# Two adapter layers over 128 samples on one core: the ends of the last two pairs of samples shared out anew between VectorE, GpSimd, ScalarE and TensorE

## The chip, the core and the metric

The program runs on one core of a Trainium2 chip. A core has TensorE (PE in the profile; its weight loads are PEld), VectorE (DVE), ScalarE (ACT), GpSimd (POOL) and SyncE (SP), which issues most of the DMAs; ScalarE can issue them too. Each engine works through its own list of instructions in order, and they wait for one another by semaphores. The metric is the device time of one execution in microseconds (us). Before the change three executions took 3142.12, 3143.81 and 3145.17 us, so the median is 3143.81 us.

## What is computed

The input x holds 128 samples of 128 rows by 1024 columns in f32, and each sample has a role that picks one of three sets of weights. Two layers of the same form follow one another:

```python
h = jnp.einsum('bsh,bhk->bsk', hidden_states, W_down[role]) + b_down[role][:, None, :]
h = jax.nn.gelu(h, approximate=False)
u = jnp.einsum('bsk,bkh->bsh', h, W_up[role]) + b_up[role][:, None, :]
y = hidden_states + u
mean = jnp.mean(y, axis=-1, keepdims=True)
var = jnp.mean(jnp.square(y - mean), axis=-1, keepdims=True)
yn = (y - mean) * jax.lax.rsqrt(var + LN_EPS)
return yn * gamma[role][:, None, :] + beta[role][:, None, :]
```

H is 1024 and K is 512. What matters here is the last part, the layer norm: a row's mean and variance, then (y - mean) * gamma * 1/sqrt(var + eps) + beta.

## The kernel before

There are four phases: down and up of layer 0, then down and up of layer 1. A phase runs over 64 items of two samples each. An item of two samples with one role computes its product in seven parts, each a product of two halves, instead of eight (Winograd's form of a 2 x 2 block product); the last item of the program is such a pair, and so is the one before it. A phase's products go into three kinds of PSUM bank, "b" (3 buffers), "e" (3) and "a" (2). ScalarE puts the bias into a bank first (`seeded`), and the products add to it with start=False.

The order of all work is written by hand. Each step is pushed on a heap with a due time in slots (`at`), an item's base being 7 slots after that of the item before; the steps are emitted in order of due time, and each engine keeps the order in which its instructions were emitted. So the due times in `finish` and `finish_last` decide what stands before what on each engine.

In the up phase the seven parts of an item are evicted on VectorE: `begin` (L629) adds a bank to x, `whole` and `end` (L635 for the last item, L638 for the others) add the second part to it and, for the others, sum the row as well. For the last item BN_STATS (L636) takes the statistics.

An item's end for all but the last (`finish`), for each of its two samples s:

- `squares`: on ScalarE the mean (L700, L702), the sum of squares (L704, an ACTIVATE over 128x1024) and the variance (L705); on GpSimd the power -1/2 of it (L706), which gives the factor v.
- `scaled`: on VectorE o = (x + mean) * gamma (L709; here "mean" is the negative mean).
- `stored`: for s = 0 o * v on ScalarE (L716) and + beta on GpSimd (L717); for s = 1 both in one instruction on VectorE (L719). Then the store of 512 KB on SP's queue.

The last item's end (`finish_last`): `total` joins the statistics (L654) and adds eps (L656) on VectorE and takes the power on GpSimd (L657); `scaled` (L660) gives o for both samples on VectorE, 1024 columns each; `stored` (L666) applies v and beta to half a sample on VectorE and stores 256 KB, for both halves of sample 1 and the right half of sample 0; `stored_beside` does the left half of sample 0 on ScalarE (L671) and GpSimd (L672), with the store on ScalarE's queue.

The item before the last is number 61 in the program's names, the last is 62. On VectorE the tail of the list, as emitted, is: L638 (61, its last part), L629 (62), L709 (61, sample 1), L635 (62, part 5), L636, L719 (61, sample 1), L635 (62, part 6), L636, L654, L656, L635 (62, part 7), L636, L654, L656, L660 twice, L666 three times. Part 7 uses the same PSUM bank as part 5, so its products wait for the eviction of part 5.

Of the kernel before, what the change touches and what calls it, by code (L numbers as in the profile page):

```python
# [26 lines left out]
def kernel(  # L27
# [57 lines left out]
    def flat(tag, bufs, name, size=2048):  # L85
        return work.tile([P, size], F32, tag=tag, name=name, bufs=bufs)
# [177 lines left out]
    def zeros(tags):  # L264
        for t in tags:
            ps = psum.tile([P, 512], F32, tag=t, name=f"{t}_zero", bufs=3)
            nc.tensor.matmul(ps, zero[:, 0:P], zero[:, P:640], start=True, stop=True)
# [55 lines left out]
    def gathered(name, values, where):  # L323

        ps = bank_a(name + "_ps")
        n = where.shape[1]
        nc.tensor.matmul(ps[0:SQ, 0:n], values, where, start=True, stop=True)
        t = const.tile([1, n], I32, name=name)
        nc.vector.tensor_copy(t, ps[0:1, 0:n])
        return t  # L330
# [15 lines left out]
    counted(own_place, key, own_key, ALU.is_gt, ones_r)  # L346
    nc.vector.tensor_copy(wide_place, own_place.to_broadcast((P, SQ)))
    place = gathered("place", wide_place, onehot)
    zeros("bbbeeebbb")

    def reg(t, s, engines, top):
# [21 lines left out]
    def result(i, y, cols, queue):  # L373


        dst = out[ds(i, 1), :, cols].rearrange("o s h -> (o s) h")
        store = queue.dma_start(dst, y).ins
        tc.declare_no_dep(store, group="result", reason="disjoint rows")
        tc.add_to_no_dep_group("result", store)
# [197 lines left out]
    class Up:  # L577
# [63 lines left out]

        whole = end

        def finish_last(self):


            mv = [const.tile([P, 3], F32, name=f"last_mv{s}") for s in range(2)]
            o = [flat("q", 4, f"o{self.tag}_{s}", H) for s in range(2)]
            row = lambda t, s, cols: t[:, ds(self.places[s], 1), cols].rearrange("p o n -> p (o n)")
            self.out_at = [reg(perm, 2 * self.n + s, [ENG.SP, ENG.Activation], B - 1) for s in range(2)]  # L650
            left, right, both = slice(0, H // 2), slice(H // 2, H), slice(0, H)

            def total(s):
                nc.vector.bn_aggr(mv[s][:, 0:2], self.stat[:, s])  # L654
                v = mv[s][:, 2:3]
                nc.vector.tensor_scalar(v, mv[s][:, 1:2], LN_EPS, None, ALU.add)  # L656
                nc.gpsimd.tensor_tensor(v, v, mhalf[:, 0:1], ALU.pow)  # L657

            def scaled(s):
                nc.vector.scalar_tensor_tensor(  # L660
                    o[s], self.x[:, s], mv[s][:, 0:1], row(self.ph.gamma, s, both), ALU.subtract, ALU.mult
                )

            def stored(s, cols, queue):
                y, v = o[s][:, cols], mv[s][:, 2:3]
                nc.vector.scalar_tensor_tensor(y, y, v, row(self.ph.beta, s, cols), ALU.mult, ALU.add)  # L666
                result(self.out_at[s], y, cols, queue)

            def stored_beside():
                y, v = o[0][:, left], mv[0][:, 2:3]  # L670
                nc.scalar.mul(y, y, v)  # L671
                nc.gpsimd.tensor_tensor(y, y, row(self.ph.beta, 0, left), ALU.add)  # L672
                result(self.out_at[0], y, left, nc.scalar)

            return [
                (10.2, lambda: total(0)),
                (12.2, lambda: total(1)),
                (12.4, lambda: scaled(0)),
                (12.5, lambda: scaled(1)),
                (12.6, lambda: stored(1, left, nc.sync)),  # L680
                (12.7, lambda: stored(1, right, nc.sync)),
                (12.8, stored_beside),
                (12.9, lambda: stored(0, right, nc.sync)),
            ]

        def finish(self):
            if self.last:
                return self.finish_last()
            steps = []
            for s in range(2):  # L690
                t = (10.4, 12.4)[s] if self.n < NPAIR else (10.9, 12.65)[s]
                one = lambda n: small.tile([P, 2], F32, tag=n, name=n + self.tag, bufs=6)
                box = {}
                row = lambda t, s=s: t[:, ds(self.places[s], 1), :].rearrange(
                    "p o n -> p (o n)"
                )

                def squares(s=s, box=box, one=one):
                    part, box["m"], box["v"] = one("part"), one("mean"), one("var")
                    nc.scalar.mul(part, self.stat[:, s], -1.0 / H)  # L700
                    m, v = box["m"][:, 0:1], box["v"][:, 0:1]
                    nc.scalar.activation(m, part[:, 0:1], AF.Identity, bias=part[:, 1:2])  # L702
                    box["o"] = flat("q", 4, f"o{self.tag}_{s}", H)
                    nc.scalar.activation(box["o"], self.x[:, s], AF.Square, bias=m, accum_out=v)  # L704
                    nc.scalar.activation(v, v, AF.Identity, bias=eps, scale=1.0 / H)  # L705
                    nc.gpsimd.tensor_tensor(v, v, mhalf[:, 0:1], ALU.pow)  # L706

                def scaled(s=s, box=box, row=row):
                    nc.vector.scalar_tensor_tensor(  # L709
                        box["o"], self.x[:, s], box["m"][:, 0:1], row(self.ph.gamma), ALU.add, ALU.mult  # L710
                    )

                def stored(s=s, box=box, row=row):
                    o, v = box["o"], box["v"][:, 0:1]
                    if s == 0:
                        nc.scalar.mul(o, o, v)  # L716
                        nc.gpsimd.tensor_tensor(o, o, row(self.ph.beta), ALU.add)  # L717
                    else:
                        nc.vector.scalar_tensor_tensor(o, o, v, row(self.ph.beta), ALU.mult, ALU.add)  # L719
                    if self.layer == 0:  # L720
                        nc.sync.dma_start(mid[self.n][s], o)
                    else:
                        i = reg(perm, 2 * self.n + s, [ENG.SP], B - 1)
                        result(i, o, slice(0, H), nc.sync)

                steps += [(t, squares), (t + 1.3, scaled), (t + 3.1, stored)]
            return steps


    SLOTS = 7  # L730
# [12 lines left out]
    for k, ph in enumerate(phases):  # L743
        for m, n in enumerate(sequence):
# [4 lines left out]
            def load(box=box, ph=ph, n=n, kind=kind, m=m):  # L749
                item = box["item"] = kind(ph, n)  # L750
                item.m = m
                item.early = ph is phases[0] and m == 0
                item.last = ph is phases[-1] and m == NI - 1
                item.among_weights = ph is phases[2] and m < 3
                if m == left_over_at + 1:
                    item.SEED = -1.65
                item.load()
# [151 lines left out]
```

## Time and profile before

| | us |
|---|---|
| median of three runs | 3143.81 |
| the profiled execution | 3143.59 |
| its span (first to last instruction) | 3141.8 |
| PE busy in the span | 3109.3 (99%) |
| DVE, POOL, ACT busy | 1977.3, 1793.9, 1203.6 |
| the last matmul's modelled end | 3128.45 |
| the last VectorE instruction's end | 3138.60 |

The times in the views below count from the span's start. A line of the timeline gives start, duration, engine, line of the code, operation and what it writes and reads; neighbours on one engine with the same line are merged (x2, x3), and in brackets stands how long the engine was idle before it and who ended that. From the last matmul to the end of the span there are 13.4 us.

### The profile page before, as it was taken

The page shows a single profiled execution, that of the slowest core. Times are in us where ns is not written, and L with a number is a line of the kernel's source. Part 1 is how long each engine was busy: PE and PEld are TensorE (multiplying, and loading weights), DVE is VectorE, ACT ScalarE, POOL GpSimd, SP SyncE. Part 2 cuts the span into 40 slices and gives each one's busy share as a digit, 9 for nine tenths or more (in the row PEclk, how much of TensorE's full clock was granted, in tenths as well). Part 3 has the DMA queues.
Part 4 walks back from the last instruction along what each step waited for, and adds up shares of the span by engine and source line. Part 5 has one row for each costly group of instructions (what it writes and reads, how often), then busy time and mean ns, then how long its engine had stood idle before and what let it go on. Part 6 is the DMA issues. An engine that isn't in the chain of part 4 may idle for free.

```text
span 3141.8 us, 42319 instructions
## 1 busy us (share of the span) xinstructions
PE 3109.3 (99%) x10806; PEld 2053.3 (65%) x10806; DVE 1977.3 (63%) x2794; ACT 1203.6 (38%) x2814; POOL 1793.9 (57%) x1396
## 2 busy tenths in 40 slices
PE   8999999999999999999999999999999999999998
PEld 6888888888544444444478888888884444444443
DVE  5655445454578777788854444444447777787777
ACT  1222222222445455555432222222224545554554
POOL 3544444444577767777654443444436777677776
PEclk9999999999999999999999999999999999999999
DMA  8888878886786666666796555555568766666665
GB/s 191 207 209 213 209 206 210 212 213 191 278 286 222 218 217 218 217 223 216 235 260 164 128 135 128 134 125 137 126 184 292 264 219 216 218 217 221 215 226 175
DMA packets 430165, 642.21 MB, mean 204 GB/s; under 512 B 36081, under 2 KB 305906, under 8 KB 428786
## 3 DMA queue, kind: packets, MB, share of 16 engines
q1 hardware_dynamic: 429458, 637.94, 69.1%
q8 instruction: 102, 1.67, 0.2%
q10 hardware_dynamic: 480, 1.57, 0.2%
q14 instruction: 125, 1.02, 0.1%
HBM read 405.01 MB, written 234.36 MB: 204 GB/s over the span
## 4 chain that ended last, share of the span: by engine, by line
PE 48%; DMA 1%; DVE 1%; issue 0%; ACT 0%; DVEq 0%; SPq 0%; ACTq 0%
PE bu L410 14%; PE bd L410 14%; PE eu L410 7%; PE ed L410 7%; PE au L410 3%; PE ad L410 3%; DMA mid<-ou 0%; DVE ou L719 0%; DMA wall<-mid 0%; DMA hd<-hd 0%; ACT ou L704 0%; DVE xu L635 0%; DVE last_stat L636 0%; DVE xu L638 0%; DVEq L905 0%
## 5 line engine op out<-in xcount | busy, mean ns | idle before, releaser
L410 PE MATMUL bu<-wall,hTu 128*128 (+1 forms) x2048 | 922.0, 592 | 2.1 <-POOL ou L717 0.7
L527 DVE STREAM_TRANSPOSE xTd<-xqd 128x1024 f32<-128x1024 f32 x250 | 505.0, 2087 | 354.1 <-PE bd L410 275.4
L410 PEld LDWEIGHTS bu<-wall,hTu 128*128 128x128 f32 x2048 | 388.7, 190 | 490.9 <-issue 455.6
L401 POOL TENSOR_TENSOR Sd<-xTd 128x512 f32<-128x512 f32 x125 | 160.5, 1284 | 802.6 <-DVE xTd L527 798.7
L706 POOL TENSOR_TENSOR varu<-varu,mhalf 128x1 f32<-128x1 f32 x254 | 333.7, 1314 | 383.1 <-ACT varu L705 383.1
L410 PE MATMUL bd<-wall,xTd 128*128 (+1 forms) x2080 | 490.9, 379 | 1.4 <-DMA wall<-T 0.8
L410 PE MATMUL eu<-wall,hTu 128*128 (+1 forms) x1040 | 488.0, 592 | 0.0
L709 DVE SCALAR_TENSOR_TENSOR ou<-xu,meanu,tables 128x1024 f32<-128x1024 f32 x254 | 327.1, 1288 | 253.3 <-ACT ou L704 253.0
L410 PE MATMUL bd<-wall,Sd 128*128 (+1 forms) x2016 | 476.5, 379 | 2.3 <-ACT hd L560 1.6
L410 PEld LDWEIGHTS bd<-wall,xTd 128*128 128x128 f32 x2080 | 394.9, 190 | 58.0 <-issue 3.5
L410 PEld LDWEIGHTS bd<-wall,Sd 128*128 128x128 f32 x2016 | 382.8, 190 | 56.7 <-issue 4.1
L565 ACT ACTIVATE hd<-hd 128x256 f32<-128x256 f32 x382 | 159.4, 418 | 536.4 <-DVE hd L564 536.4
L410 PEld LDWEIGHTS eu<-wall,hTu 128*128 128x128 f32 x1040 | 197.6, 190 | 247.5 <-issue 229.6
L700 ACT ACTIVATE partu<-statu 128x2 f32<-128x2 f32 x254 | 51.9, 204 | 730.6 <-DVE xu L638 730.6
L717 POOL TENSOR_TENSOR ou<-ou,tables 128x1024 f32<-128x1024 f32 x127 | 299.5, 2358 | 0.1
L704 ACT ACTIVATE ou<-xu,meanu 128x1024 f32<-128x1024 f32 x254 | 292.2, 1150 | 8.3
L410 PE MATMUL ed<-wall,xTd 128*128 (+1 forms) x1072 | 254.6, 381 | 4.8 <-DVE xTd L402 4.8
L401 POOL TENSOR_TENSOR hTu<-hTu 128x256 f32<-128x256 f32 x126 | 205.3, 1630 | 66.3 <-DVE hTu L607 54.4
L410 PE MATMUL ed<-wall,Sd 128*128 (+1 forms) x1008 | 238.2, 379 | 0.1
L410 PE MATMUL ad<-wall,xTd 128*128 (+1 forms) x1008 | 238.2, 379 | 0.0
L410 PE MATMUL au<-wall,hTu 128*128 (+1 forms) x504 | 236.8, 592 | 0.0
L410 PEld LDWEIGHTS ed<-wall,xTd 128*128 128x128 f32 x1072 | 204.5, 191 | 33.6 <-issue 5.6
(114 smaller groups left out, 3349.8 us busy)
## 6 DMA issues: line engine op xcount, KB each, us to landing
xqd<-in_x_dram SPq DMA_DIRECT2D x512, 128.0 KB, 3.3
hd<-hd SPq DMA_DIRECT2D x256, 256.0 KB, 2.4
xu<-in_x_dram SPq DMA_DIRECT2D x128, 512.0 KB, 5.0
mid<-ou SPq DMA_DIRECT2D x128, 512.0 KB, 6.1
xu<-mid SPq DMA_DIRECT2D x128, 512.0 KB, 5.8
out_dram<-ou SPq DMA_DIRECT2D x126, 512.0 KB, 5.5
hqu<-hd SPq DMA_DIRECT2D x244, 256.0 KB, 6.5
xqd<-mid SPq DMA_DIRECT2D x488, 128.0 KB, 3.8
```

What stands on the lines that cost most here:

```text
L401: engine.tensor_tensor(dst[:, 1], a11, a21, ALU.subtract)
L410: nc.tensor.matmul(ps[:, 0:cols], a[:, j], w.rhs(r, j, cols), start=start and j == 0, stop=j == n - 1, skip_group_check=True,)
L527: nc.vector.transpose(self.a[:, s].rearrange("p j (t a) -> p j a t", t=SQ), self.xq[s].rearrange("p a (i j) -> p j a i", i=SQ),)
L565: nc.scalar.activation(y, y, AF.Gelu)
L700: nc.scalar.mul(part, self.stat[:, s], -1.0 / H)
L704: nc.scalar.activation(box["o"], self.x[:, s], AF.Square, bias=m, accum_out=v)
L706: nc.gpsimd.tensor_tensor(v, v, mhalf[:, 0:1], ALU.pow)
L709: nc.vector.scalar_tensor_tensor(box["o"], self.x[:, s], box["m"][:, 0:1], row(self.ph.gamma), ALU.add, ALU.mult)
L717: nc.gpsimd.tensor_tensor(o, o, row(self.ph.beta), ALU.add)
```

## The change

The `scaled` and `stored` steps of the last two items are shared out differently.

- Item 61, sample 0: `stored` runs on VectorE in one instruction (L763 after), no longer on ScalarE and GpSimd.
- Item 61, sample 1: (x + mean) runs on ScalarE (L750) and * gamma on GpSimd (L751). For v and beta, ScalarE makes a 128x128 matrix with v on its diagonal (L681, from `same`, an identity matrix made once at the program's start), copies beta into two PSUM banks (L686), and TensorE multiplies the diagonal matrix with each half of o and adds it to the bank (L690). ScalarE copies the two banks back into o (L691) and stores 512 KB on its own queue.
- Item 62, sample 0, left half: `scaled` is done for this half alone on VectorE (L665), then the same three steps follow: a third bank with beta, a second diagonal matrix, one product, one copy and a store of 256 KB on ScalarE's queue.
- Item 62, the rest: `scaled` for sample 1 (1024 columns), its two halves stored, then `scaled` and `stored` for the right half of sample 0, all on VectorE (L665, L672), stores on SP's queue as before.

After the change the tail of VectorE's list is: L640 (61, its last part), L631 (62), L763 (61, sample 0), L637 (62, part 5), L638, L637 (part 6), L638, L659, L661, L637 (part 7), L638, L659, L661, L665 (62, sample 0 left), L665 (sample 1), L672 twice, L665 (sample 0 right), L672. On GpSimd the tail is L746 twice (61's powers), L751, L662 twice. On ScalarE it is L745, L750, L681, L686 three times, L681, L691 twice, a store, L691, a store. TensorE gets the three products after part 7 of item 62. The lists of all engines are otherwise as before, but for `same` at the start of VectorE's.

```diff
--- before.py
+++ after.py
@@ -346,6 +346,8 @@
     counted(own_place, key, own_key, ALU.is_gt, ones_r)
     nc.vector.tensor_copy(wide_place, own_place.to_broadcast((P, SQ)))
     place = gathered("place", wide_place, onehot)
+    same = const.tile([P, P], F32, name="same")
+    nc.vector.tensor_scalar(same, iota_row, iota_col, None, ALU.is_equal)
     zeros("bbbeeebbb")
 
     def reg(t, s, engines, top):
@@ -641,14 +643,17 @@
 
         whole = end
 
+        def row(self, t, s, cols=slice(0, H)):
+            return t[:, ds(self.places[s], 1), cols].rearrange("p o n -> p (o n)")
+
         def finish_last(self):
 
 
             mv = [const.tile([P, 3], F32, name=f"last_mv{s}") for s in range(2)]
-            o = [flat("q", 4, f"o{self.tag}_{s}", H) for s in range(2)]
-            row = lambda t, s, cols: t[:, ds(self.places[s], 1), cols].rearrange("p o n -> p (o n)")
+            o = []
             self.out_at = [reg(perm, 2 * self.n + s, [ENG.SP, ENG.Activation], B - 1) for s in range(2)]
             left, right, both = slice(0, H // 2), slice(H // 2, H), slice(0, H)
+            diagonal, begun = {}, {}
 
             def total(s):
                 nc.vector.bn_aggr(mv[s][:, 0:2], self.stat[:, s])
@@ -656,30 +661,65 @@
                 nc.vector.tensor_scalar(v, mv[s][:, 1:2], LN_EPS, None, ALU.add)
                 nc.gpsimd.tensor_tensor(v, v, mhalf[:, 0:1], ALU.pow)
 
-            def scaled(s):
+            def scaled(s, cols):
                 nc.vector.scalar_tensor_tensor(
-                    o[s], self.x[:, s], mv[s][:, 0:1], row(self.ph.gamma, s, both), ALU.subtract, ALU.mult
+                    o[s][:, cols], self.x[:, s, cols], mv[s][:, 0:1], self.row(self.ph.gamma, s, cols),
+                    ALU.subtract, ALU.mult,
                 )
 
             def stored(s, cols, queue):
                 y, v = o[s][:, cols], mv[s][:, 2:3]
-                nc.vector.scalar_tensor_tensor(y, y, v, row(self.ph.beta, s, cols), ALU.mult, ALU.add)
+                nc.vector.scalar_tensor_tensor(y, y, v, self.row(self.ph.beta, s, cols), ALU.mult, ALU.add)
                 result(self.out_at[s], y, cols, queue)
 
-            def stored_beside():
-                y, v = o[0][:, left], mv[0][:, 2:3]
-                nc.scalar.mul(y, y, v)
-                nc.gpsimd.tensor_tensor(y, y, row(self.ph.beta, 0, left), ALU.add)
-                result(self.out_at[0], y, left, nc.scalar)
+            def room():
+                o.extend(flat("q", 4, f"o{self.tag}_{s}", H) for s in range(2))
+                t = flat("s", 3, "diagonal", 1792)
+                diagonal.update(before=t[:, 0:P], last=t[:, P : 2 * P])
+
+            def on_diagonal(name, v):
+                nc.scalar.mul(diagonal[name], same, v)
+
+
+            def begin_bank(item, s, cols, t):
+                begun[item.n, cols.start] = ps = bank(t, f"{item.tag}_end{cols.start}")
+                nc.scalar.copy(ps, item.row(item.ph.beta, s, cols))
+
+            def by_tensor(item, y, name, cols):
+                ps = begun[item.n, cols.start]
+                nc.tensor.matmul(ps, diagonal[name], y[:, cols], start=False, stop=True, skip_group_check=True)
+                nc.scalar.copy(y[:, cols], ps)
+
+            def begin_banks():
+                begin_bank(before_last[0], 1, left, "b")
+                begin_bank(before_last[0], 1, right, "e")
+                begin_bank(self, 0, left, "b")
+
+            def end_before():
+                item, box = before_last
+                for cols in (left, right):
+                    by_tensor(item, box["o"], "before", cols)
+                i = reg(perm, 2 * item.n + 1, [ENG.Activation], B - 1)
+                result(i, box["o"], both, nc.scalar)
+
+            def end_left():
+                by_tensor(self, o[0], "last", left)
+                result(self.out_at[0], o[0][:, left], left, nc.scalar)
 
             return [
+                (8.6, room),
+                (8.8, lambda: on_diagonal("before", before_last[1]["v"][:, 0:1])),
+                (9, begin_banks),
                 (10.2, lambda: total(0)),
+                (12.05, lambda: on_diagonal("last", mv[0][:, 2:3])),
+                (12.1, end_before),
                 (12.2, lambda: total(1)),
-                (12.4, lambda: scaled(0)),
-                (12.5, lambda: scaled(1)),
+                (12.3, lambda: scaled(0, left)),
+                (12.4, end_left),
+                (12.5, lambda: scaled(1, both)),
                 (12.6, lambda: stored(1, left, nc.sync)),
                 (12.7, lambda: stored(1, right, nc.sync)),
-                (12.8, stored_beside),
+                (12.8, lambda: scaled(0, right)),
                 (12.9, lambda: stored(0, right, nc.sync)),
             ]
 
@@ -691,9 +731,9 @@
                 t = (10.4, 12.4)[s] if self.n < NPAIR else (10.9, 12.65)[s]
                 one = lambda n: small.tile([P, 2], F32, tag=n, name=n + self.tag, bufs=6)
                 box = {}
-                row = lambda t, s=s: t[:, ds(self.places[s], 1), :].rearrange(
-                    "p o n -> p (o n)"
-                )
+                row = lambda t, s=s: self.row(t, s)
+                if self.before_last and s == 1:
+                    before_last[:] = [self, box]
 
                 def squares(s=s, box=box, one=one):
                     part, box["m"], box["v"] = one("part"), one("mean"), one("var")
@@ -706,13 +746,17 @@
                     nc.gpsimd.tensor_tensor(v, v, mhalf[:, 0:1], ALU.pow)
 
                 def scaled(s=s, box=box, row=row):
+                    if self.before_last and s == 1:
+                        nc.scalar.activation(box["o"], self.x[:, s], AF.Identity, bias=box["m"][:, 0:1])
+                        nc.gpsimd.tensor_tensor(box["o"], box["o"], row(self.ph.gamma), ALU.mult)
+                        return
                     nc.vector.scalar_tensor_tensor(
                         box["o"], self.x[:, s], box["m"][:, 0:1], row(self.ph.gamma), ALU.add, ALU.mult
                     )
 
                 def stored(s=s, box=box, row=row):
                     o, v = box["o"], box["v"][:, 0:1]
-                    if s == 0:
+                    if s == 0 and not self.before_last:
                         nc.scalar.mul(o, o, v)
                         nc.gpsimd.tensor_tensor(o, o, row(self.ph.beta), ALU.add)
                     else:
@@ -723,8 +767,13 @@
                         i = reg(perm, 2 * self.n + s, [ENG.SP], B - 1)
                         result(i, o, slice(0, H), nc.sync)
 
-                steps += [(t, squares), (t + 1.3, scaled), (t + 3.1, stored)]
+                steps += [(t, squares), (t + 1.3, scaled)]
+
+                if not (self.before_last and s == 1):
+                    steps.append((t + (3.2 if self.before_last else 3.1), stored))
             return steps
+
+    before_last = []
 
 
     SLOTS = 7
@@ -751,6 +800,7 @@
                 item.m = m
                 item.early = ph is phases[0] and m == 0
                 item.last = ph is phases[-1] and m == NI - 1
+                item.before_last = ph is phases[-1] and m == NI - 2
                 item.among_weights = ph is phases[2] and m < 3
                 if m == left_over_at + 1:
                     item.SEED = -1.65
```

## The prediction

> **What bounds the kernel now.** I read the page first, for which engine sets the time, and then the last 20 us alone, since the change touches nothing else but one instruction at the start.
>
> ```profile
> PE 3109.3 (99%) x10806; PEld 2053.3 (65%) x10806; DVE 1977.3 (63%) x2794; ACT 1203.6 (38%) x2814; POOL 1793.9 (57%) x1396
> ```
>
> TensorE is the bound of the whole, and the change removes none of its products. What it can shorten is the end, after TensorE has nothing left to cover the other engines. The timeline of the end, a choice of lines:
>
> ```profile
> 3124.53 1.28 DVE L709 SCALAR_TENSOR_TENSOR ou<-xu,meanu,tables 128x1024 f32<-128x1024 f32 x1 [1.27 <-ACT ou L704]
> ...
> 3125.73 0.68 DVE L635 TENSOR_TENSOR xu<-bu,xu 128x512 f32<-128x512 f32 x1
> 3126.19 2.35 POOL L717 TENSOR_TENSOR ou<-ou,tables 128x1024 f32<-128x1024 f32 x1
> 3126.45 0.69 DVE L636 BATCH_NORM_STATS2 last_stat<-xu 128x6 f32<-128x512 f32 x1
> ...
> 3126.47 1.98 PE L410 MATMUL bu<-wall,hTu 128*128 x4 [0.56 <-DVE xu L635]
> ...
> 3127.06 2.56 DVE L719 SCALAR_TENSOR_TENSOR ou<-ou,varu,tables 128x1024 f32<-128x1024 f32 x1
> ...
> 3129.55 0.68 DVE L635 TENSOR_TENSOR xu<-eu,xu 128x512 f32<-128x512 f32 x1
> ...
> 3131.30 0.68 DVE L635 TENSOR_TENSOR xu<-bu,xu 128x512 f32<-128x512 f32 x1
> ...
> 3133.12 2.48 DVE L660 SCALAR_TENSOR_TENSOR ou<-xu,last_mv,tables 128x1024 f32<-128x1024 f32 x2
> ...
> 3135.29 1.43 POOL L672 TENSOR_TENSOR ou<-ou,tables 128x512 f32<-128x512 f32 x1 [0.48 <-ACT ou L671]
> 3135.71 2.89 DVE L666 SCALAR_TENSOR_TENSOR ou<-ou,last_mv,tables 128x512 f32<-128x512 f32 x3
> 3136.75 0.40 ACTq L377 DMA_DIRECT2D out_dram<-ou  x1
> ```
>
> Three losses are to be seen. VectorE waits 1.27 us for ScalarE before L709, and the eviction of part 5 (3125.73) stands behind it, so TensorE waits 0.56 us. L719 takes 2.56 us where it takes 1.25 to 1.32 elsewhere (its minimum and median before 3120): it ends 1.1 us after L717 does. The first L666 takes 1.56 us and the other two 0.74 (so its own line's view says): it runs beside L672. And parts 6 and 7, whose products were done at 3125.9 and 3128.45, are evicted at 3129.55 and 3131.30. So from 3125.73 on VectorE's list alone sets the end, as the chain of waits says too, whose last line is
>
> ```profile
> 3137.93 0.66 DVE ou L666
> ```
>
> The windows of 1 us show what lies behind it (engines' busy time, then clock, DMA share, GB/s):
>
> ```profile
> 3130.00:3131.00 1.00, 0.00 (x0) 0.00 (x0) 0.93 (x3) 0.00 (x0) 0.00 (x0) 0.75 1.00 393
> ...
> 3138.00:3139.00 1.00, 0.00 (x0) 0.00 (x0) 0.59 (x1) 0.00 (x0) 0.00 (x0) 0.50 1.03 385
> 3139.00:3140.00 1.00, 0.00 (x0) 0.00 (x0) 0.00 (x0) 0.00 (x0) 0.00 (x0) 0.50 1.04 383
> 3140.00:3141.00 1.00, 0.00 (x0) 0.00 (x0) 0.00 (x0) 0.00 (x0) 0.00 (x0) 0.50 0.42 158
> ```
>
> Stores move about 385 GB/s, the last byte comes at 3140.4, and 1.4 us later the span ends: 3.2 us after VectorE's last instruction.
>
> [...] L719 and L666 (o and the table) are held to the end of L717 and L672; L635 and L636 beside L717 keep 0.68 and 0.69 us. [...] The kernel's biases already work so, at 0.57 us for a copy of 512 columns (L428). [...] Here it goes from 1.00 to 0.75 and 0.50 in the windows from 3130 on, some 2 us after its last product. [...] The three 1 us windows from 3138 move 0.93 MB of both queues together.
>
> **The change, part by part.** I rebuild the end from step lengths in this trace, start to start: L635 to L636 0.72 us, L636 to L654 0.73, L654 to L656 0.24, L656 to L660 0.13, L656 to L635 0.07, L666 to L666 0.67 (512 columns), L660 to L660 1.20 (1024), L660 to the L666 that reads it 1.39, so a dependent step costs 0.19 more.
>
> *Up to part 5's eviction.* L709 goes from VectorE, and with it the 1.27 us wait. In its place comes L763 for sample 0 of item 61. Its o is ready at 3122.04 (L709's first one, 3120.76 + 1.28), its v at 3122.46 (L706, 3121.14 + 1.32), both before L629 ends at 3123.26. So L763 runs 3123.2 to 3124.5. Part 5's products (3122.31, the last at 3123.60, modelled 0.59) are done by 3124.2, so L637 starts at 3124.45: 1.28 us earlier. What queues behind L763 is this eviction, so part 7 and the end: the new wait is for GpSimd's power, with 0.7 us to spare.
>
> *TensorE.* Part 6 starts at 3124.03 as before and takes 4 x 0.43 = 1.72; part 7 then follows at 3125.75 without the wait, modelled end 3127.63 (0.8 us earlier).
>
> *Parts 6 and 7.* L719 and its stall are gone from VectorE. Part 6 can be evicted at 3125.95, then L638 3126.67, L659 3127.40, L661 3127.64. Part 7's eviction follows at 3127.75, not 3131.30. Of the 3.55 us won here 1.28 were counted above, so this is 2.27.
>
> *The last steps.* From there: L638 3128.47, L659 3129.20, L661 3129.44, L665 left half of sample 0 3129.57, L665 sample 1 3130.24, L672 twice at 3131.63 and 3132.30, L665 right half 3132.97, L672 on it 3133.83, end 3134.57 (0.74). That is 6.82 us from part 7's eviction, where before it was 7.30: one L660 of 1.20 becomes two of 0.67, one dependent step adds 0.19, the 0.82 us block by L672 goes. Sum for VectorE: 1.28 + 2.27 + 0.48 = 4.03 us, end at 3134.57 for 3138.60.
>
> *GpSimd and ScalarE beside it.* L750 like L716, 1.13 us: 3124.73 to 3125.87. L751 like L717, 2.35: 3125.95 to 3128.30[...]. The diagonal matrix isn't in the trace; between an ACTIVATE of two columns (L700, 0.20) and 512 columns (L671, 0.72) I take 0.4. Three copies of beta, 0.52 apart, end by 3127.8. The power L662 follows L751, so 3128.9, the second diagonal 3129.35. Hidden, all of it.
>
> *The products.* The start of the program shows that a product of 512 f32 columns is two matmuls of 0.43 us (the zero products of L267: 3 calls, x6), so 0.86 and 0.16 more to its modelled end. 61's halves: 3128.35 to 3129.4, and to 3130.2. Copies back, 0.57 each (PSUM to SBUF for 256 columns is 0.37, L560; 256 columns into PSUM cost the same): 3130.0 and 3130.8. A register load (0.29) and the issue (0.40): the 512 KB start by 3131.5. The third product waits for L665 (3130.3), ends 3131.3, is copied by 3132.2 and issued by 3132.7. Against the last store on SP (3134.6) this has about 1.9 us to spare. At half clock each product takes 1.71 us: the issue is then at about 3135.1, and 0.5 us are lost.
>
> *Stores.* Before, 1 MB followed in the last 2 us of issues; now there are 512 KB and four times 256 KB (1.57 MB) issued from 3131.5 to 3134.6. With data 0.95 us after an issue (3136.75 to 3137.7 before) at 385 GB/s the last byte comes at 3136.4, the span ends 1.4 us later: 3137.8. `same` at the start (0.29, like L277) falls into VectorE's wait of 3.77 us for the first bias, so it is free; without that cover it costs its 0.29 us.
>
> So the span goes from 3141.8 to 3137.8. The profiled execution was 3143.59, 1.8 us more than its span, so it would be 3139.6; the median is 0.2 above it: 3139.8 us, 0.13% faster. A measurement of this kernel tells about 0.2% (6.3 us) from no change, and the shown runs spread over 3 us.
>
> **Rivals.**
>
> *The gain is smaller, about 2.7 us (3141.1).* L661 could be excluded by L751 (to 3128.3: 0.6 us late), the products could run at half clock (0.5), and the stores could go at the 292 GB/s of the busiest slice of the page: 1.57 MB take 5.4 us from 3132.3, so the end is at 3139.1. Against it: no small VectorE instruction in the shown end is held by GpSimd, and the stores alone moved 385.
>
> *Nothing is gained (3143.8, within 1 us).* L719's stall would be one that other executions don't have. Against it: another L719, at 3114.55, takes 2.41 us.
>
> *Slower: GpSimd's power in front of the last product.* Place: L763 at 3123.2, before part 5's eviction. Price: each us that the power of item 61 is later than 3123.2 delays part 7 and all behind it by as much. It decides from 0.7 + 4.0 = 4.7 us of delay, and the time would be 3144.8 at 5.7. For it: GpSimd is in order and L706's powers stand behind L717 of item 60. Against: that one ends at 3115.87.
>
> *More gained than 0.2%.* VectorE needs 6.8 us after part 7 and TensorE can't end earlier, so only chance in the measurement brings this: 3137.2.
>
> **How the numbers follow.** Forecast 0.56, smaller gain 0.24, nothing 0.06, slower 0.04, more than 0.2% 0.10. The range goes from 3137.6 (the forecast with half of the runs' spread and some 0.7 us of step lengths) to 3142.8 (the smaller gain with the same spread). The forecast's own range is 3138.3 to 3141.2. Faster by over 0.2%: 0.10; slower: 0.04; between: 0.86.
>
> **What would show it.** Right: part 7's matmuls without idle time before them; part 7's eviction some 3.5 us earlier; no VectorE instruction above 1.3 us in the last 15; ScalarE's second store issued before SP's last. Wrong: L763 waiting for GpSimd, a long L661, a product that takes 1.7 us, a last byte more than 2 us after the last issue, or a difference in the 3100 us before the end.

## The result, and the profile after

| | median of runs, us | runs |
|---|---|---|
| before, beside it | 3144.57 | 22 |
| after | 3140.40 | 22 |

The ratio is 0.9987 with a 95% interval of 0.9982 to 0.9993: some 4 us faster, 0.13%. One of the 22 runs of after took 8687.84 us, for a reason that no trace shows; it is left out of the ratio, and without it the median is 3140.34. The profiled execution of after took 3142.18 us, its span 3139.98. That execution is on the slow side of the median by 1.8 us, and the reason lies not in the tail, as will be seen. So the tail is measured here from a point inside it: the first product of part 6 of item 62, the last group of products that writes an "e" bank (`eu`) before the end. The distance from there to the end of the span is called the tail below. Before, part 6 started at 3124.03 and the span ended at 3141.82: 17.79 us. After, 3126.57 and 3139.98: 13.41 us.

The busy line of the page of after:

```profile
PE 3115.3 (99%) x10812; PEld 2056.7 (65%) x10812; DVE 1976.0 (63%) x2795; ACT 1204.9 (38%) x2821; POOL 1788.3 (57%) x1395
```

TensorE is still the bound of the whole. Its count is up by six: three products of two matmuls each. The timeline of after's end, a choice of lines (start, duration, engine, line, operation, what it writes and reads, idle time before it):

```profile
3125.71 1.28 DVE L763 SCALAR_TENSOR_TENSOR ou<-ou,varu,tables 128x1024 f32<-128x1024 f32 x1
3126.57 1.88 PE L412 MATMUL eu<-wall,hTu 128*128 x4
3126.90 0.68 DVE L637 TENSOR_TENSOR xu<-bu,xu 128x512 f32<-128x512 f32 x1
...
3128.29 1.88 PE L412 MATMUL bu<-wall,hTu 128*128 x4
...
3128.47 2.35 POOL L751 TENSOR_TENSOR ou<-ou,tables 128x1024 f32<-128x1024 f32 x1 [0.49 <-ACT ou L750]
...
3130.19 0.15 DVE L661 TENSOR_SCALAR last_mv<-last_mv 128x1 f32<-128x1 f32 x1
3130.26 0.68 DVE L637 TENSOR_TENSOR xu<-bu,xu 128x512 f32<-128x512 f32 x1
...
3130.88 1.13 PE L690 MATMUL bu_end<-ou,diagonal 128*128 128x512 f32 x2 [0.71 <-POOL ou L751]
...
3134.14 1.41 DVE L672 SCALAR_TENSOR_TENSOR ou<-ou,last_mv,tables 128x512 f32<-128x512 f32 x2
3134.74 0.38 ACTq L379 DMA_DIRECT2D out_dram<-ou  x1
...
3136.25 0.75 DVE L672 SCALAR_TENSOR_TENSOR ou<-ou,last_mv,tables 128x512 f32<-128x512 f32 x1
```

Part 7 (3128.29) follows part 6 after 1.72 us, with no idle time in brackets; before there were 0.56 us of it. The eviction of part 7 (3130.26) comes 3.69 us after the start of part 6; before, it came 7.27 us after it. L763, which is queued in front of part 5's eviction (3126.90), shows no wait. No VectorE instruction is held: the two L672 take 1.41 us together, where a single one had taken 1.56 beside GpSimd. ScalarE's second store is issued at 3134.74, VectorE's last instruction starts at 3136.25.

The windows of 1 us of after's last stretch (engines' busy time, then clock, DMA share, GB/s):

```profile
3134.00:3135.00 1.00, 0.08 (x1) 0.00 (x0) 0.90 (x3) 0.59 (x1) 0.00 (x0) 1.00 0.63 250
3135.00:3136.00 1.00, 0.00 (x0) 0.00 (x0) 1.00 (x2) 0.00 (x0) 0.00 (x0) 1.00 0.98 377
3136.00:3137.00 1.00, 0.00 (x0) 0.00 (x0) 0.96 (x2) 0.00 (x0) 0.00 (x0) 1.00 1.01 377
3137.00:3138.00 1.00, 0.00 (x0) 0.00 (x0) 0.00 (x1) 0.00 (x0) 0.00 (x0) 1.00 0.96 350
3138.00:3139.00 1.00, 0.00 (x0) 0.00 (x0) 0.00 (x0) 0.00 (x0) 0.00 (x0) 0.76 0.59 219
```

From 3135 to 3138 the stores run at 350 to 377 GB/s without a gap, so the bytes may now set the end about as much as VectorE does; the last two experiments ask that. The last byte moves at about 3138.7, and the span ends 1.28 us later.

### The profile page after: what moved, and what is told of

It is laid out like the page before. It is cut to its first block, busy times and chain, and to the rows that moved or that the text cites. A ratio compares the mean times of both kernels' runs of the same rounds, so it can differ in the third digit from the quotient of the medians.

```text
span 3140.0 us, 42344 instructions
## 1 busy us (share of the span) xinstructions
PE 3115.3 (99%) x10812; PEld 2056.7 (65%) x10812; DVE 1976.0 (63%) x2795; ACT 1204.9 (38%) x2821; POOL 1788.3 (57%) x1395
## 3 DMA queue, kind: packets, MB, share of 16 engines
q14 instruction: 125, 1.02, 0.1%
## 5 line engine op out<-in xcount | busy, mean ns | idle before, releaser
L746 POOL TENSOR_TENSOR varu<-varu,mhalf 128x1 f32<-128x1 f32 x254 | 333.3, 1312 | 382.2 <-ACT varu L745 382.2
L403 POOL TENSOR_TENSOR hTu<-hTu 128x256 f32<-128x256 f32 x126 | 202.9, 1610 | 68.5 <-DVE hTu L609 53.5
```

Source lines behind the costliest of these rows:

```text
L403: engine.tensor_tensor(dst[:, 1], a11, a21, ALU.subtract)
```

## Experiments

All traces are compared by the tail. "To VectorE" is the time from part 6 to the end of VectorE's last instruction. The ratios are to the kernel before, run on the same chip beside each. A tail is read from one trace of each kernel; the three traces with after's end agree to 0.01 us.

| kernel | tail | to VectorE | median | ratio, 95% |
|---|---|---|---|---|
| before | 17.79 | 14.56 | | |
| after | 13.41 | 10.43 | 3140.40 | 0.9987 (0.9982–0.9993) |
| after again | 13.40 | 10.43 | 3140.41 | 0.9989 (0.9982–0.9995) |
| item 61 alone | 14.36 | 11.18 | 3141.32 | 0.9991 (0.9984–0.9998) |
| item 62 alone | 16.97 | 13.99 | 3143.16 | 0.9996 (0.9988–1.0005) |
| no product for 61 | 16.07 | 13.06 | 3141.95 | 0.9994 (0.9985–1.0002) |
| order alone | 18.28 | 15.06 | 3144.47 | 1.0001 (0.9993–1.0010) |
| more to TensorE | 14.36 | 9.51 | 3140.77 | 0.9988 (0.9982–0.9995) |
| the same, stores spread | 14.21 | 9.64 | 3140.56 | 0.9991 (0.9984–0.9997) |
| TensorE busy at the boundary | 13.41 | 10.43 | 3141.01 | 0.9988 (0.9982–0.9995) |

By time alone, item 62 alone, no product for 61 and order alone can't be told from before, since their intervals include 1: for these three the tail is the evidence.

My theory was that the 4 us are VectorE's: its list alone sets the end, and three holds in it go (the wait before L709, the blocked L719, the blocked first L666). One rival was that a change of the order on VectorE would do as well, by setting TensorE's part 7 free. The other was that the work only had to leave VectorE, whoever takes it, so that the products with diagonal matrices add nothing.

### Item 61 alone

The last item keeps its end as it was before (against after):

```diff
-                begin_bank(self, 0, left, "b")
...
-                (12.05, lambda: on_diagonal("last", mv[0][:, 2:3])),
...
-                (12.3, lambda: scaled(0, left)),
-                (12.4, end_left),
+                (12.4, lambda: scaled(0, both)),
...
-                (12.8, lambda: scaled(0, right)),
+                (12.8, stored_beside),
```

> The change for item 61 alone; the last item ends as before. Measure: the tail, from the first matmul of part 6 of item 62 to the end of the span (before 17.77 us, after 13.43). My theory: item 61's work in front of and between VectorE's last evictions was the loss, so most of the gain stays: tail 14.0 us (after plus 0.56 for two products of 1024 columns and the block by GpSimd's addition), up to 15 if GpSimd's addition is shut out by VectorE's three last instructions. Rival, that the last item's own path decides: tail 17 us or more.

Measured: a tail of 14.36 us. From item 61 comes 3.43 us of the 4.38. Its two moves (sample 0 onto VectorE, sample 1 off it) weren't run apart. The timeline shows what stays (the second fence is the same timeline of VectorE's middle L672 alone):

```profile
3132.51 3.08 DVE L672 SCALAR_TENSOR_TENSOR ou<-ou,last_mv,tables 128x512 f32<-128x512 f32 x3
3132.69 1.70 POOL L707 TENSOR_TENSOR ou<-ou,tables 128x512 f32<-128x512 f32 x1 [1.07 <-ACT ou L706]
```

```profile
3133.18 1.75 DVE L672 SCALAR_TENSOR_TENSOR ou<-ou,last_mv,tables 128x512 f32<-128x512 f32 x1
```

The first L672 runs from 3132.51 to about 3133.26 and GpSimd's addition comes at 3132.69; it gets in after the first L672, and the second is held to 3134.93. That is a loss of 1.0 us against the 0.75 of an undisturbed one (the addition itself took 1.70 us, where one of this size takes 1.28 undisturbed): the block of the kernel before, with another instruction as its victim.

### Item 62 alone

The reverse: item 61 ends as before.

```diff
-                begin_bank(before_last[0], 1, left, "b")
-                begin_bank(before_last[0], 1, right, "e")
...
-                (8.8, lambda: on_diagonal("before", before_last[1]["v"][:, 0:1])),
...
-                (12.1, end_before),
...
-                    if self.before_last and s == 1:
-                        nc.scalar.activation(box["o"], self.x[:, s], AF.Identity, bias=box["m"][:, 0:1])
-                        nc.gpsimd.tensor_tensor(box["o"], box["o"], row(self.ph.gamma), ALU.mult)
-                        return
...
-                    if s == 0 and not self.before_last:
+                    if s == 0:
...
```

> The change for item 62 alone; item 61 ends as before. My theory: tail 17.2 us (before less 0.56), a median about 0.5 us below before, which times can't show. Rival, that the last item's own path decides: tail 15.5 us or less.

Measured: 16.97 us. The wait and the block are both still in its timeline:

```profile
3125.57 1.28 DVE L745 SCALAR_TENSOR_TENSOR ou<-xu,meanu,tables 128x1024 f32<-128x1024 f32 x1 [1.27 <-ACT ou L740]
...
3128.10 2.56 DVE L755 SCALAR_TENSOR_TENSOR ou<-ou,varu,tables 128x1024 f32<-128x1024 f32 x1
```

The two halves of the change bring 3.43 and 0.82 us, together 4.25; the whole brings 4.38. They add up to within 0.13 us: neither hides the other. One thing differs inside: without the products for item 61, TensorE stood idle for 5.56 us before the last item's product, which then ran at clock 0.50 and took 2.04 us for the 1.10 of after.

### No product for item 61

Sample 1 of item 61 leaves VectorE as in after, but v goes on by ScalarE and beta by GpSimd, without the banks and the products:

```diff
...
-                for cols in (left, right):
-                    by_tensor(item, box["o"], "before", cols)
+                nc.scalar.mul(box["o"], box["o"], box["v"][:, 0:1])
+                nc.gpsimd.tensor_tensor(box["o"], box["o"], item.row(item.ph.beta, 1), ALU.add)
...
```

> As after, but sample 1 of item 61 gets its factor from ScalarE and its beta from GpSimd, with no diagonal matrix and no product. My theory: GpSimd's addition of 2.35 us and VectorE's last products exclude each other, and the power for the last sample stands behind it: tail 16.3 us (15.5 to 16.8), so the product is what makes the new division pay. Rival, that only the order and the removal from VectorE matter: tail 13.4 to 13.9 us.

Measured: 16.07 us, so 2.66 of the 4.38 us are lost again. The chain stands in the timeline:

```profile
3130.84 3.34 POOL L699 TENSOR_TENSOR ou<-ou,tables 128x1024 f32<-128x1024 f32 x1 [1.55 <-ACT ou L698]
...
3134.15 0.54 POOL L662 TENSOR_TENSOR last_mv<-last_mv,mhalf 128x1 f32<-128x1 f32 x1
...
3134.73 1.41 DVE L672 SCALAR_TENSOR_TENSOR ou<-ou,last_mv,tables 128x512 f32<-128x512 f32 x2 [2.74 <-POOL last_mv L662]
```

Here it is GpSimd that is held: its addition takes 3.34 us where one of this size takes 2.35 undisturbed. Behind it in GpSimd's list stands the power of the last item, and VectorE waits 2.74 us for that. So the second rival falls for this arrangement: leaving VectorE is not enough when the work goes to GpSimd here, and the product that adds o * v to beta in PSUM takes it off both. Of the 2.66 us the hold is 0.99; the rest comes from the power's place behind the addition. A kernel with the power in front of the addition was not run, so what the product is worth against the best division without it stays open.

### The order alone

Against the kernel before: L709's step is only emitted later, so that part 5 is evicted in front of it.

```diff
-                steps += [(t, squares), (t + 1.3, scaled), (t + 3.1, stored)]
+                later_on = 1.4 if self.before_last and s == 1 else 0
+                steps += [(t, squares), (t + 1.3 + later_on, scaled), (t + 3.1, stored)]
```

> The kernel before with one move: the product of x and gamma for sample 1 of item 61 on VectorE stands behind the eviction and statistics of part 5. TensorE's idle time of 0.56 us before part 7 goes away. My theory: VectorE's list decides, and the instruction for sample 1 of item 61 then meets GpSimd's addition later: tail 17.8 to 18.6 us, no gain. Rival, that TensorE's wait is what counts: tail 17.0 us.

Measured: 18.28 us, half a microsecond longer than before. TensorE's idle time is gone (part 7 starts 1.72 us after part 6), and nothing is won by it:

```profile
3126.32 3.10 POOL L717 TENSOR_TENSOR ou<-ou,tables 128x1024 f32<-128x1024 f32 x1 [0.49 <-ACT ou L716]
...
3127.34 3.17 DVE L719 SCALAR_TENSOR_TENSOR ou<-ou,varu,tables 128x1024 f32<-128x1024 f32 x1
```

VectorE's list has the same work in it, and both engines are now held by each other: 3.10 us for 2.35, and 3.17 for 1.28. The first rival falls too, for the order that was run; other orders of VectorE's list were not.

### After once more

> The changed kernel once more, beside the next two on one chip. My theory: tail 13.4 us as in its first trace, wherever the span ends. In its first trace TensorE ran at half clock for 3.4 us after an idle time of 2.02 us at 1606, and came to part 6 2.5 us later than before; where that does not happen, part 6 starts near 3124.5 and the span is about 3138. Rival, that the change itself delays the work ahead of the tail: part 6 again at 3126 or later, each time.

Measured: 13.40 us, part 6 at 3124.64, span 3138.04. So the tail is the same to 0.01 us, and the start of part 6 at 3126.57 in the first trace of after is no property of the kernel. Where it came from: up to 1607 us the products of before and after start at the same times to about 0.3 us, and by 1613.3 after is 2.7 us behind (the group after the two shown below starts at 1613.31, that of before at 1610.64). That is the boundary between the layers. TensorE's timeline of after there:

```profile
1608.09 2.53 PE L412 MATMUL bd<-wall,Sd 128*128 128x256 f32 x8 [2.02 <-ACT hd L562]
1610.42 3.05 PE L412 MATMUL bd<-wall,xTd 128*128 128x256 f32 x8
```

The same groups in the trace of before:

```profile
1607.11 1.97 PE L410 MATMUL bd<-wall,Sd 128*128 128x256 f32 x8 [1.24 <-ACT hd L560]
1608.91 1.89 PE L410 MATMUL bd<-wall,xTd 128*128 128x256 f32 x8
```

TensorE waits there for a copy on ScalarE, which itself waits for a DMA to land (for 7.11 us in before, 7.9 in after). In after's first trace it stood idle 2.02 us instead of 1.24, and then eight matmuls took 3.05 us instead of 1.89. The window of after says why:

```profile
1610.00:1612.00 2.00, 2.00 (x6) 1.62 (x5) 0.51 (x2) 1.79 (x6) 1.92 (x2) 0.50 1.10 267
```

The granted clock is 0.50. In the second trace of after the idle time was 1.63 us and the clock stayed at 1.00.

### TensorE kept busy at the boundary

Five small products (ten matmuls) whose result nobody uses, placed in that idle time:

```diff
+    def keep_warm():
+        ps = bank_a("warm_ps")
+        for _ in range(5):
+            nc.tensor.matmul(ps[:, 0:P], same, same, start=True, stop=True)
+
+    at(SLOTS * 2 * NI + 17.5, keep_warm)
```

> After, with five extra products of the identity matrix with itself (about 1.1 us, result unused) for TensorE before the wait at 1606 in layer 1's first phase. Theory that the half clock there makes the spread: idle time there at most 1.2 us, no half clock between 100 and 3100 us, median 0.5 to 1.2 us below that of after beside it, and a narrower spread. Rival, that the spread comes from the waits for DMAs there: median and spread as after, or the median up to 1.1 us later.

```profile
1605.33 1.28 PE L902 MATMUL warm_ps<-same 128*128 128x128 f32 x10
1607.03 1.97 PE L412 MATMUL bd<-wall,Sd 128*128 128x256 f32 x8 [0.42 <-ACT hd L562]
```

The timeline shows that the products fill the gap (0.42 us idle), the clock stays at 1.00, and the span of this trace, 3137.24, is the shortest of all ten. But the median of 21 runs is 3141.0, against 3140.4 for after on the same chip, and the standard deviation is 1.20 us against 1.32. A median 0.5 to 1.2 us lower was expected, so this was a miss. The half clock makes a single trace longer, after's first by 1.69 us; that it makes up the spread of the runs is not shown, and this run speaks against it.

### More to TensorE, twice

If VectorE's list still set the end, then taking more from it should shorten the tail. Sample 1 of item 61 is done in halves, each stored by itself on SP's queue, and the right half of the last item's sample 0 is also finished by a product:

```diff
+                begin_bank(self, 0, right, "e")
...
+                (12.05, lambda: end_before(left)),
+                (12.1, lambda: on_diagonal("last", mv[0][:, 2:3])),
+                (12.15, lambda: end_before(right)),
...
+                (12.3, lambda: scaled(0, both)),
+                (12.4, lambda: end_first(left)),
+                (12.45, lambda: end_first(right)),
...
-                (12.8, lambda: scaled(0, right)),
-                (12.9, lambda: stored(0, right, nc.sync)),
```

> After, with two more moves: the gamma product, the bank copy and the store of sample 1 of item 61 in two halves, and the right half of sample 0 of item 62 by TensorE and ScalarE too. My theory: in after the last stores follow one another without a gap from 3134.4 on and VectorE ends at the same time, so both must move: VectorE ends 0.9 us earlier, the stores start 1.5 us earlier, tail 12.9 us (12.6 to 13.2). Rival, that ScalarE becomes the last: its fourth copy and store end later than in after, tail 13.4 us or more.

Measured: VectorE ended 0.92 us earlier, and the tail was 0.95 us longer. This was a miss, and the timeline and the windows show how:

```profile
3134.26 1.10 PE L690 MATMUL bu_end<-ou,diagonal 128*128 128x512 f32 x2 [1.63 <-DVE ou L665]
...
3136.49 0.59 ACT L691 COPY ou<-eu_end 128x512 f32<-128x512 f32 x1 [0.51 <-PE eu_end L690]
3137.11 0.38 ACTq L379 DMA_DIRECT2D out_dram<-ou  x1
```

```profile
3135.00:3136.00 1.00, 1.00 (x3) 0.19 (x1) 0.90 (x2) 0.59 (x1) 0.00 (x0) 1.00 0.00 0
3136.00:3137.00 1.00, 0.22 (x1) 0.00 (x0) 0.83 (x2) 0.51 (x1) 0.00 (x0) 1.00 0.04 14
3137.00:3138.00 1.00, 0.00 (x0) 0.00 (x0) 0.00 (x0) 0.08 (x1) 0.00 (x0) 1.00 1.02 377
3138.00:3139.00 1.00, 0.00 (x0) 0.00 (x0) 0.00 (x0) 0.00 (x0) 0.00 (x0) 0.75 1.02 383
```

The products of the last item wait for the whole of L665 on sample 0 (1.63 us), so the DMA engines have nothing to move from 3135 to 3137. Then four stores of 256 KB come at once, 1.05 MB, which take 2.8 us at 380 GB/s. VectorE had already ended at 3136.83. So the rival held: ScalarE's last store is issued 9.79 us after part 6, in after 8.17. But only 0.42 of the 0.95 us are the bytes' (the last one comes 12.55 us after part 6, in after 12.13). The other 0.53 us lie behind them: the span ends 1.80 us after the last byte instead of 1.28.

So the same again, with the left half of L665 first once more, and one of ScalarE's stores put on SP:

```diff
-                (12.3, lambda: scaled(0, both)),
-                (12.4, lambda: end_first(left)),
-                (12.45, lambda: end_first(right)),
+                (12.3, lambda: scaled(0, left)),
+                (12.35, lambda: scaled(0, right)),
+                (12.4, lambda: end_first(left, nc.sync)),
+                (12.45, lambda: end_first(right, nc.scalar)),
```

> As the kernel with two more moves, but the left half of sample 0 of item 62 comes first on VectorE again and its store goes to SP's queue, so that no store issue stands in front of ScalarE's last copy. My reading of that kernel's trace (no byte moved from 3135 to 3137, then four stores of 256 KB at 380 GB/s): the last megabyte of stores is the floor. With results from about 8.1 us after part 6's start on, the last byte comes at 11.8 to 12.0 us as in after, tail 13.2 to 13.5 us: no gain left here. Rival, that ScalarE's queue was the loss there: VectorE's earlier end shows, tail 12.5 us.

Measured: the last byte comes 12.06 us after part 6, close to the 11.8 to 12.0 expected and to the 12.13 of after. The tail of 14.21 us was a miss, 0.7 us above its range. The windows of this kernel, with part 6 at 3124.39:

```profile
3132.00:3133.00 1.00, 0.75 (x2) 0.00 (x0) 0.90 (x2) 0.73 (x2) 0.00 (x0) 1.00 0.00 0
3133.00:3134.00 1.00, 0.00 (x0) 0.00 (x0) 1.00 (x2) 0.38 (x1) 0.00 (x0) 1.00 0.65 240
3134.00:3135.00 1.00, 0.00 (x0) 0.00 (x0) 0.03 (x1) 0.00 (x0) 0.00 (x0) 1.00 0.84 305
3135.00:3136.00 1.00, 0.00 (x0) 0.00 (x0) 0.00 (x0) 0.00 (x0) 0.00 (x0) 1.00 1.04 383
3136.00:3137.00 1.00, 0.00 (x0) 0.00 (x0) 0.00 (x0) 0.00 (x0) 0.00 (x0) 1.00 0.33 121
3137.00:3138.00 1.00, 0.00 (x0) 0.00 (x0) 0.00 (x0) 0.00 (x0) 0.00 (x0) 0.82 0.00 0
```

VectorE ends 0.79 us earlier than in after and the bytes hardly at all. The last four stores, 1.05 MB, begin at 3133.4, after more than a microsecond in which no byte moved, and take 3.1 us from there to 3136.44. So in this kernel the end of the bytes is set by when the first of these stores is ready and by the bytes that follow, not by VectorE's last instruction. The tail is 14.21 us because the span ended 2.16 us after the last byte instead of 1.28. SP's first wait to end after it ends 0.85 us later here, 0.40 in after; why is open. The median, 3140.56, isn't below that of after, and no kernel run here is measurably faster than after.

## Why the prediction was right

It said 3139.8 us, 4.0 below before; the median is 3140.4, 4.2 below that of before beside it. Its sum had three terms for VectorE. Measured in the two traces from the start of part 6:

| term | predicted | measured | from |
|---|---|---|---|
| up to part 5's eviction | 1.28 | 1.37 | 1.70 before, 0.33 after |
| from there to part 7's eviction | 2.27 | 2.21 | 5.57 before, 3.36 after |
| the last steps | 0.48 | 0.56 | 7.30 before, 6.74 after |
| VectorE's end | 4.03 | 4.14 | 14.56 before, 10.43 after (differences of rounded times) |

- **The wait that goes.** L763 was to start 0.83 us before part 6 and started 0.86 before it. The new wait, for GpSimd's power, didn't come up; the rival with the slower end needed it 4.7 us late.
- **What TensorE was to bring.** Part 7 without idle time is as predicted. But the run with the order alone shows that this is no gain by itself: the gain is that VectorE gets to part 7 earlier. The prediction had said that VectorE's list sets the end, and counted part 7's 0.8 us in no sum of its own.
- **The blocks.** The prediction called L719's 2.56 us a block by L717, with L635 and L636 unhindered beside it at 0.68 and 0.69. The three runs that bring such a pair together, a SCALAR_TENSOR_TENSOR of o or x with a table on VectorE and an addition of beta on GpSimd, show it again (1.75 for 0.75; 3.34 for 2.35; 3.10 and 3.17 for 2.35 and 1.28), and the end of after, where no such pair meets, has none: beside L751, L637, L638 and L661 took 0.69, 0.69 and 0.15 us. That settles the rival "nothing is gained" too: in the run with item 62 alone the block is there again at 2.56 us. One reading beside it was too narrow: 1.25 to 1.32 us for L719 elsewhere holds for about the last 400 us before 3120 only. Over all its 126 executions before 3120 the least is 1.24, the median 1.47 and the most 2.41 us. Of the 127 with the last one, 84 take over 1.32 us, and every one of these starts while an L717 runs: the block goes through both up phases.
- **The smaller gain.** Of its three grounds none held in after. L661 took 0.15 us beside L751 in the middle of its run. The three products ran at full clock (1.13, 1.02 and 1.10 us for two matmuls with the modelled end). The stores moved 377 GB/s, not 292. The half clock was a real danger, though: in the two runs without the products for item 61 the last item's product took 2.04 and 2.05 us at clock 0.50 (the prediction's 1.71 was an estimate, twice its 0.86). In after, with those products in front of it, TensorE was idle for at most 0.71 us between part 7 and the last product, and the clock was 1.00 (see the last section).
- **The hidden work.** The diagonal matrix took 0.38 and 0.40 us for the estimate of 0.4, a copy out of PSUM 0.59 for 0.57. ScalarE's second store was issued 8.17 us after part 6, 0.5 earlier than predicted, and 1.5 us before VectorE's last instruction even started.
- **The filled bank.** When the prediction says that the biases already work so, this is what they do: ScalarE copies them into a bank, and the products go into it with start=False, as the three products here do with beta. Each copy of 512 columns of beta took 0.57 us (L686), as those of the biases do. This kernel also writes its "b" and "e" banks with products of zeros at the start (L267, 18 matmuls into `b_zero` and `e_zero`). No run leaves them out, so whether they are needed here is not shown.
- **The end.** Last byte 12.1 us after part 6 for 12.4, end of the span 1.28 us later for 1.4, tail 13.41 for 13.77.
- **Outside the span.** The prediction left the 1.8 us between span and time as they were. In the runs of after they are 2.1 on average, so 0.3 us of the gain are lost there. The average is as high, 2.0 to 2.15, in the four experiments whose ScalarE stores the 512 KB of item 61 (item 61 alone, no product, after once more, TensorE busy at the boundary), and 1.8 in the four others; why is open.

That the absolute time came within 0.6 us is in part luck. In the second trace of after the tail is 0.4 us shorter than predicted, part 6 comes 0.6 later and the time outside the span is 0.3 longer; and part 6 starts anywhere from 3123.83 to 3127.32 in the ten traces. What the traces bear out are the terms of the sum, not the last digit.

Three things were off without harm. The prediction set part 6 at 3124.03 "as before". In the one trace of after it was 2.5 us later, from the layer boundary; in the second trace 0.6. And it named "a difference in the 3100 us before the end" as a sign that it was wrong. Such a difference did appear, and it belongs to the execution and not to the change, as the second trace shows. The prediction also priced the last item's part at 0.48 us of VectorE's time. Alone it brings 0.57 (14.56 to 13.99), but with item 61 already changed it brings 0.75 (11.18 to 10.43), since without it the block by GpSimd moves to the second L672.

## What to carry to other kernels

At the end of a kernel, where the bound engine has run out of work, look for the list of one engine that sets the end, and in it for instructions that take longer than the same ones elsewhere. Moving them to GpSimd only moved the hold here (its addition took 3.34 us for 2.35), and put the work in front of a small step that VectorE waited 2.74 us for; a product with a diagonal matrix on a TensorE that has nothing left to do took a scale and an addition off both. Once that list is short enough, look at the bytes of the last stores: here it mattered when they were ready, and not which engine finished first. And compare single traces from a point inside the stage that was changed: here a longer idle time 1500 us earlier, with the half clock behind it, shifted one of them by 2.5 us, more than half of the gain.

## What was not expected of the hardware

**When the clock fell.** At the layer boundary of these ten traces the granted clock fell after idle times of 1.92, 2.02 and 2.12 us and not after those of 0.42 to 1.86 us. The clock in windows of 2 us there:

| trace | idle, us | 1606:1608 | 1608:1610 | 1610:1612 | 1612:1614 |
|---|---|---|---|---|---|
| item 62 alone | 2.12 | 0.74 | 0.50 | 0.91 | 1.00 |
| after | 2.02 | 1.00 | 0.84 | 0.50 | 0.81 |
| more to TensorE | 1.92 | 1.00 | 0.83 | 0.50 | 0.82 |
| item 61 alone | 1.86 | 1.00 | 1.00 | 1.00 | 1.00 |
| the same, stores spread | 1.66 | 1.00 | 1.00 | 1.00 | 1.00 |
| after again | 1.63 | 1.00 | 1.00 | 1.00 | 1.00 |
| no product for 61 | 1.40 | 1.00 | 1.00 | 1.00 | 1.00 |
| order alone | 1.40 | 1.00 | 1.00 | 1.00 | 1.00 |
| before | 1.24 | 1.00 | 1.00 | 1.00 | 1.00 |
| TensorE busy at the boundary | 0.42 | 1.00 | 1.00 | 1.00 | 1.00 |

That looks like a border at 1.9 us of idle time, but the idle time alone does not explain it. By the shares in these windows the half clock set in only 0.5, 1.3 and 0.8 us after the products had begun again (in the order 1.92, 2.02, 2.12) and lasted 3.4 us each time. And after the last product of the program the clock stayed at 1.00 for 2.05 us in before and for 4.93 in the second trace of after. What decides when it falls is not shown.

At the end it fell in front of a product in two traces. Without the products for item 61, TensorE stood idle for 5.56 us (item 62 alone) and 2.81 us (no product for 61), the clock fell at 3132.72 and 3130.76, and the next product ran at half clock. In after, where those products follow part 7 with 0.71 us of idle time, the clock stays at 1.00 to the end of the last product and 4.4 us beyond it.

In the first trace of after the 16 matmuls took 5.22 us (1608.09 to 1613.31) where before they took 3.53 (1607.11 to 1610.64): 1.69 us for the half clock, beside 0.78 us of longer waiting.

**How long a hold is.** In the ends of these traces there are eleven places where a VectorE SCALAR_TENSOR_TENSOR of 512 or 1024 columns with a table and GpSimd's addition of beta meet. In every one the later instruction takes longer by what was left of the other, less a constant. For GpSimd as the later one this constant is 0.16 us (five places, with 0.31 to 1.14 us left), for VectorE 0.20 (six places, with 1.02 to 2.09 us left). So L719 in before starts when L717 has 1.48 us left, and takes 1.28 us longer than its 1.28. GpSimd's power of one column is not counted there; beside L665 it took 1.06 us in after, where the one before it took 0.55. With VectorE instructions back to back, GpSimd's addition still got in between two: in the run with item 61 alone it came at 3132.69, in the middle of the first of three, and took 1.70 us for 1.28, and the second took 1.75 for 0.75.

**The time after the last byte.** The span ended 1.27 or 1.28 us after it in eight of the ten traces, and 1.80 and 2.16 us after it in the two with more on TensorE. Which step makes the difference is open.
